# A graph network's second aggregation pair: transposes, own rows and product order rearranged

## The chip, the cores and the metric

The kernel runs on one core of a Trainium2 chip. The metric is the device time of one execution in microseconds (us). One execution was also recorded by the hardware profiler; the profile and the trace are of that execution.

A core has a matrix engine (TensorE, PE in the profile; PEld is its loading of stationary operands), a vector engine (VectorE, DVE), an activation engine (ScalarE, ACT), GpSimd (POOL) and SyncE (SP). Each runs its own list of instructions in order and waits on semaphores for the others. On this kernel SP only issues transfers, and POOL issues the indirect transfers that gather rows. Products are summed in PSUM banks, and an engine has to evict a bank before TensorE may use it again.

## The reference

The input is x (2708 x 512) and a sparse weighted adjacency matrix adj (2708 x 2708, nonzero diagonal). There are four residual layers, each fed by a layer norm. Layer 2, which the change concerns, is a pair of graph convolutions and a dense layer:

```python
h = relu(layernorm(x))
h = relu(adj @ (h @ W1) + b1)
h = relu(adj @ (h @ W3) + b3)
x = x + tanh(h @ Wf + bf)
```

Layer 3 then normalises x, applies relu and `@ W + b`, and averages the result over the nonzero pattern of adj. Layer 0 averages over an incidence matrix, and layer 1 is masked attention over the neighbours.

## The kernel before

Rows are worked on in 22 row tiles of 128 (the last has 20 rows and is called the tail). Low-numbered rows have many neighbours, so each row tile's aggregate is cut in two. WHOLE[m] leading column tiles are multiplied as dense blocks (6 for tiles 0 to 5, 4 or 3 for tiles 6 to 20). The remaining neighbours are listed: CHUNKS[m] chunks of up to 128 columns, whose source rows POOL gathers into eight buffers (L1032) and whose weights are read as `ac` (L1025). Dense blocks are split into a high part, a low part and a sum (a_hi on ACT at L1070, a_lo and a_s on VectorE at L1071 and L1072), so that three quick products each (L1083) give enough precision. A listed chunk is one slow product (L1086). Tile 0 takes all columns as blocks, tile by tile (L1098).

For each row tile of layer 2 the kernel does this:

- Aggregate into two banks, agg (the high products) and aggs (mixed).
- Evict with a bias into u: two VectorE operations at L1117. For tiles 6 to 20 the diagonal is treated alone: the bias is first the tile's own rows times a diagonal weight: SP loads them into u (L1109), VectorE scales them and adds the bias (L1110).
- relu_parts transposes u in four products (L972) and makes v_hi (ACT, L977), v_lo and v_s (VectorE, L978 and L981).
- project3 multiplies these with a weight, in 12 products (L997), into the banks main and mixed, of which there is one each.

There are two loops over row tiles. Stage A (625 to 903 us) is the first aggregation: its projection with W3 is evicted into `go` and stored as g2d, from which the second aggregation gathers. It also stores marks (nz) of what is nonzero, which layer 3 reads. Stage B (903 to 1310 us) aggregates from g2d, projects with Wf, adds bf, applies tanh, and adds the layer's input (L1393 to L1402) to get x after layer 2. It normalises that into z (L189 to L199), transposes z through relu_parts too, projects it with layer 3's W, and stores hid and hidr (L1410, L1413). The adding of a row's own share is L1421. Stage B visits tile 0, 3 to 9, the tail (the tile before 10 in both loops), 10 to 20, and then 1 and 2. Layer 3 follows, from 1310 us; its gathers read hidr, and its masks are the nz marks, read back at L1268.

Each loop body is written for one tile from beginning to end. The order on every engine is decided at build time by a scheduler that moves instructions of neighbouring tiles past each other, within what buffers allow: the pool wp keeps two buffers of each name, among them u (which serves the aggregate, z and the tail's x), v_hi, v_lo, v_s and go; ap keeps two of ac and a_hi, a_lo, a_s; marks have three. TensorE's order before has the eight transposes of one tile's u and an earlier tile's z side by side behind the first dense products of the next tile, and both projections inside them.

Of the kernel before, what the change touches and what calls it, by code (L numbers as in the profile page):

```python
# [14 lines left out]
U8 = mybir.dt.uint8  # L15
# [29 lines left out]
def kernel(  # L45
# [36 lines left out]
    NB = (N + BLK - 1) // BLK  # L82
    UNIT = 4
    assert N % UNIT == 0
    NCH = 8 * ((max(CHUNKS) + 7) // 8)
    NCA = max(CHUNKS)
    NCL = max(CHUNKS[LEAD:])
# [63 lines left out]
    flag = const.tile([P, 1], I32, name="flag")  # L151


    idx_g = const.tile([P, NT, NCH], U32, name="idx_g")

    rdeg = const.tile([P, NT], FP, name="rdeg")
    diag_c, self_w = (const.tile([P, NT], FP, name=name) for name in ("diag_c", "self_w"))
# [81 lines left out]
    with tc.tile_pool(name="l0_slab", bufs=2) as slabs, tc.tile_pool(  # L239
# [177 lines left out]
        def search(m):  # L417

            first = dense_of(m) * P
            num = N - first  # L420
            ranks = ranks_of.pop(m)

            end = wp.tile([P, 1], FP, name="end")
            nc.vector.tensor_scalar_add(end, ranks[:, num - 1 : num], 1.0)
            nc.vector.tensor_copy(ranks[:, num : num + 1], end)
            want = wp.tile([P, NCH], FP, name="want")
            nc.vector.tensor_scalar(want, places, end, None, op0=ALU.min)
            for c0 in range(0, CHUNKS[m], 8):
                c = slice(c0, c0 + 8)
                at = wp.tile([P, 8], U32, name="found")  # L430
                nc.vector.max_index(at, want[:, c], ranks)
                nc.vector.tensor_scalar(
                    idx_g[:, m, c],
                    at,
                    float(N - first),
                    float(first),
                    op0=ALU.min,
                    op1=ALU.add,
                )
                node = wp.tile([P, 8], FP, name="node")  # L440
                nc.vector.tensor_scalar(
                    node,
                    at,
                    float(N - 1 - first),
                    float(N // UNIT),
                    op0=ALU.min,
                    op1=ALU.mult,
                )
                nc.vector.tensor_scalar_add(
                    idx_a[:, m, c], node, float((first * N + m * P) // UNIT)  # L450
                )
            nc.vector.tensor_scalar(
                bad[:, BAD_MANY + m : BAD_MANY + m + 1],
                end,
                float(CHUNKS[m] * P + 1),
                None,
                op0=ALU.is_gt,
            )
# [189 lines left out]
        def gather_rows(m):  # L648

            gs = []  # L650
            for c in range(CHUNKS[m]):
                g = hp.tile([P, D], FP, name=f"h{DENSE + gather_slot[0] % NGG}")
                gather_slot[0] += 1
                nc.gpsimd.indirect_dma_start(  # L654
                    out=g,
                    out_offset=None,
                    in_=h0d[:, :],
                    in_offset=bass.IndirectOffsetOnAxis(ap=idx_g[:, m, c : c + 1], axis=0),
                )
                gs.append(g)  # L660
            gathers[m] = gathers[m], gs
# [282 lines left out]
    order_2 = order_m[:1] + order_m[HEAD:] + order_m[1:HEAD]  # L944
    x3_last = dram.tile([P, D], FP, name="x3_last")

    idx_h = gp.tile([P, NT, NCA], U32, name="idx_h")
    NMARK = DENSE + NCA
    gather_slot = [0]

# [12 lines left out]
    def sum_banks_scaled(dst, main, mixed, n):  # L963

        nc.scalar.activation(dst[:n], main[:n], AF.Copy, scale=SHIFT - 1.0)
        nc.vector.tensor_tensor(dst[:n], mixed[:n], dst[:n], ALU.add)

    def relu_parts(v, n):

        pt = ps_t.tile([P, NCD, P], FP, name="pt")  # L970
        for c in range(NCD):
            nc.tensor.transpose(pt[:, c, :n], v[:n, c * P : (c + 1) * P], ident[:n, :n])  # L972
        hi, lo, s = (
            wp.tile([P, NCD, P], FR, name=f"v_{part}") for part in ("hi", "lo", "s")
        )
# [10 lines left out]
    def project3(parts, n, w, pool=None, names=("main", "mixed")):  # L986

        hi, lo, s = parts
        whi, wlo, ws = w
        main, mixed = ((pool or ps_p).tile([P, D], FP, name=name) for name in names)  # L990
        for acc, a, b, first, last in (
            (main, hi, whi, True, False),
            (main, lo, wlo, False, True),
            (mixed, s, ws, True, True),
        ):
            for c in range(NCD):
                nc.tensor.matmul(  # L997
                    acc[:n],
                    a[:, c, :n],
                    b[:, c, :],  # L1000
                    start=first and c == 0,
                    stop=last and c == NCD - 1,
                )
        return main, mixed

# [15 lines left out]
        return raw[:k, : len(ts), :n], k  # L1021

    def load_listed(m):
        ac = ap.tile([P, NCA, P], FP, name="ac")[:, : CHUNKS[m], : rows(m)]
        nc.sync.dma_start(out=ac, in_=listed[m])  # L1025
        return ac

    def gather(m, gd, gs=None, index=idx_g):

        gs = gs or [gathered() for _ in range(CHUNKS[m])]  # L1030
        for c in range(CHUNKS[m]):
# [1 line left out]
                out=gs[c],  # L1033
                out_offset=None,
                in_=gd[:, :],
                in_offset=bass.IndirectOffsetOnAxis(ap=index[:, m, c : c + 1], axis=0),
            )
        return gs

    def aggregate(m, parts, shifted, gd, marked):  # L1040


        n = rows(m)
# [8 lines left out]
        mixed = ps_a.tile([P, D], FP, name="aggs")  # L1052
        chunks = []
        if num:
            ac = load_listed(m)
            chunks = [(ac[:, c, :], g) for c, g in enumerate(gather(m, gd))]
            if marked:
                mark(whole, ac)
        for ts in ([t for t in ts if t < whole] for ts in dense):
# [15 lines left out]
            for i, t in enumerate(ts):  # L1075
                ghi, glo, gs_ = gs[i]
                first, last = t == 0, t == whole - 1
                for acc, a, b, st, sp in (
# [1 line left out]
                    (main, lo, glo, False, last),  # L1080
                    (mixed, s, gs_, first, False),
                ):
                    nc.tensor.matmul(acc[:n], a[:k, i, :n], b[:k], start=st, stop=sp)  # L1083
        if chunks:
            for c, (a, g) in enumerate(chunks):
                nc.tensor.matmul(  # L1086
                    mixed[:n],
                    a,
                    g,
                    start=(c == 0 and not dense_of(m)),  # L1090
                    stop=(c == len(chunks) - 1),
                )
        else:
            for ts in others:
                gs = [shifted(t) for t in ts]
                raw, k = load_piece(m, ts)
                for i, t in enumerate(ts):
                    nc.tensor.matmul(  # L1098
                        mixed[:n], raw[:, i, :], gs[i][:k], start=False, stop=(t == NT - 1)
                    )  # L1100
        if marked:
            nc.sync.dma_start(out=nonzero[m], in_=nz[:, : whole + num, :n])
        return main, mixed

    def aggregated(m, parts, shifted, gd, bias, marked=False):
        n = rows(m)
        u = wp.tile([P, D], FP, name="u")
        if alone(m):
            nc.sync.dma_start(out=u, in_=gd[span(m)])  # L1109
            nc.vector.scalar_tensor_tensor(  # L1110
                u, u, diag_c[:, m : m + 1], bias, op0=ALU.mult, op1=ALU.add
            )
            bias = u
        main, mixed = aggregate(m, parts, shifted, gd, marked)
        if dense_of(m):
            for bank, scale in ((main, 1.0 - EPS12), (mixed, EPS12)):
                nc.vector.scalar_tensor_tensor(  # L1117
                    u[:n], bank[:n], scale, bias[:n], op0=ALU.mult, op1=ALU.add
                )
                bias = u  # L1120
        else:
            nc.vector.scalar_tensor_tensor(
                u[:n], mixed[:n], EPS12, bias[:n], op0=ALU.mult, op1=ALU.add
            )
        return relu_parts(u, n)

    def g_parts(t):
        return [gp.tile([P, D], FR, name=f"g{part}{t}") for part in ("hi", "lo", "s")]
# [53 lines left out]
    w3 = split_w(wsetb, wr, "wb")  # L1182
    wr = load_w(wset, wf_d, "wr")

    for m in order_m:
        n = rows(m)
        parts = aggregated(m, first_parts, first_product, g1d, bias1, marked=True)
        if m == 0:
            wf = split_w(wset, wr, "wa")
            wr = load_w(wset, w_d, "wr")  # L1190
        main, mixed = project3(parts, n, w3)
        go = wp.tile([P, D], FP, name="go")
        sum_banks_scaled(go, main, mixed, n)
        nc.sync.dma_start(out=g2d[span(m)], in_=go[:n])

    bf = load_bias(bf_d, "bias0")
    bl = load_bias(b_d, "bias2")
# [66 lines left out]
    def gather_h(m):  # L1264
# [1 line left out]
        whole, num = dense_of(m), CHUNKS[m]  # L1266
        nz = marks[m] = ap.tile([P, NMARK, P], U8, name="nz", bufs=3)
        nc.sync.dma_start(out=nz[:, : whole + num, : rows(m)], in_=nonzero[m])  # L1268
        gd, index = (hidr, idx_h) if whole else (hid, idx_g)
        listed_h[m] = gather(m, gd, [next(places_h) for _ in range(num)], index)  # L1270

    def bank_h(m):
        if m not in banks:
# [30 lines left out]
    def listed_products(m):  # L1304
        n = rows(m)
        whole, num = dense_of(m), CHUNKS[m]
        mask = ap.tile([P, NCA, P], FR, name="ac")[:, :num, :n]
        nc.scalar.copy(mask, marks[m][:, whole : whole + num, :n])
        for c, g in enumerate(listed_h.pop(m)):
            high = part_room()  # L1310
# [64 lines left out]
    FIRST = 2  # L1375
    EARLY, FINAL = [list(range(HEAD, DENSE)), list(range(HEAD - 1))], [[HEAD - 1]]
    assert order_2[-1] == HEAD - 1
    for m in order_2:
        n = rows(m)
        parts = aggregated(m, second_parts, second_product, g2d, bias3)  # L1380
        if m == 0:
            w = split_w(wsetb, wr, "wb")
        if dense_of(m) and m not in FULL:
            nc.vector.tensor_scalar_add(
                idx_h[:, m, : CHUNKS[m]], idx_g[:, m, : CHUNKS[m]], float(-HEAD * P)
            )
        if m == order_2[-1]:
            for k in order_3[:FIRST]:
                gather_h(k)
        main, mixed = project3(parts, n, wf)  # L1390
        z = wp.tile([P, D], FP, name="u")
        sum_banks(z, main, mixed, n)
        nc.vector.tensor_add(z[:n], z[:n], bf[:n])  # L1393
        nc.scalar.activation(z[:n], z[:n], AF.Tanh)
        if m == NFULL:
            xt = wp.tile([P, D], FP, name="u")
        else:

            place = {order_2[-1]: "gs0", NSLOT: f"slot{order_2[-1]}"}.get(m, f"slot{m}")
# [3 lines left out]
        if m == NFULL:  # L1403
            nc.sync.dma_start(out=x3_last[:n], in_=xt[:n])
        norm(wp, xt, n, z)
        main, mixed = project3(relu_parts(z, n), n, w)
        go = wp.tile([P, D], FP, name="go")
        sum_banks(go, main, mixed, n)
        nc.vector.tensor_add(go[:n], go[:n], bl[:n])
# [9 lines left out]
            halves[m] = hi, lo  # L1419
        if alone(m):  # L1420
            nc.vector.scalar_tensor_tensor(  # L1421
                xt, go, self_w[:, m : m + 1], xt, op0=ALU.mult, op1=ALU.add
            )

# [460 lines left out]
```

## Time and profile before

| what | value |
|---|---|
| three runs, median (lowest, highest) | 1452.55 us (1449.79, 1455.3) |
| the profiled execution's own time | 1455.42 us |
| its span in the trace | 1453.6 us |
| mean TensorE clock granted | 0.927 of full speed |
| busy: TensorE, VectorE, ScalarE, GpSimd | 85%, 66%, 46%, 45% of the span |
| transfers, mean over the span | 241 GB/s |
| stage A, stage B, layer 3 | 278, 407, 144 us of the span |

The profile's page sums busy time by engine, draws the span in 40 slices, and groups instructions by line. The trace can be asked for the waits of an engine (who was waited for, for how long, how often), for busy time in any stretch, for the chain of work that ended last, and for a timeline of single instructions. TensorE's records have modelled ends that overlap, so its pace is read from the distance between starts: 0.2275 us for a quick 128 x 512 product at full clock, 0.43 at half clock, and 0.857 for a listed chunk, which takes two passes.

### The profile page before, as it was taken

What the parts mean: (1) busy time and instruction counts of PE and PEld (TensorE: products, weight loads), DVE (VectorE), ACT (ScalarE), POOL (GpSimd) and SP (SyncE); (2) the same over time, 40 slices, a digit from 0 to 9 for tenths busy, and PEclk for the clock granted to TensorE, in tenths of its full rate; (3) what the DMA queues carried; (4) which work ended last, traced back from release to release, by engine and by line L of the source; (5) the groups of instructions that cost most, each with busy time, mean ns of one, the idle gap of its engine ahead of it and who ended that gap; (6) DMA issues with size and microseconds to landing.
All of it is one profiled execution on the core that took longest, in us unless ns stands there. A gap on an engine that the chain in (4) does not pass through costs nothing. (4 is left out here: it accounts for less than half of the span.)

```text
span 1453.6 us, 15184 instructions
## 1 busy us (share of the span) xinstructions
PE 1239.6 (85%) x4223; PEld 726.9 (50%) x4223; DVE 954.4 (66%) x2043; ACT 675.0 (46%) x1056; POOL 660.7 (45%) x674
## 2 busy tenths in 40 slices
PE   4888879888778569989998989899988888966997
PEld 2333334334333156655554556466645555555675
DVE  4686998788998478643443356356666656556776
ACT  5875467376344455432312224244444434435563
POOL 1245467666653431055463532334533232265773
PEclk9979999899889779999999989999999999978998
DMA  9989989899794497377776876756746555568995
GB/s 350 341 271 279 304 298 299 304 309 336 220 340 164 152 310 259 103 240 245 253 246 218 265 247 214 259 190 212 215 146 192 155 152 166 167 185 299 275 304 165
DMA packets 187750, 350.68 MB, mean 241 GB/s; under 512 B 22818, under 2 KB 96496, under 8 KB 183925
## 3 DMA queue, kind: packets, MB, share of 16 engines
q1 hardware_dynamic: 140057, 202.48, 41.8%
q0 software_dynamic: 46032, 145.05, 31.3%
q10 hardware_dynamic: 1568, 2.10, 0.4%
q8 instruction: 35, 0.57, 0.2%
q14 instruction: 58, 0.48, 0.1%
HBM read 285.96 MB, written 63.58 MB: 240 GB/s over the span
## 5 line engine op out<-in xcount | busy, mean ns | idle before, releaser
L1032 POOL DMA_INDIRECT gg<-g2d,idx_g x130 | 133.0, 1023 | 242.3 <-PE aggs L1086 199.1
L1086 PE MATMUL aggs<-gg,ac 128*128 128x512 f32 (+1 forms) x520 | 235.8, 595 | 4.7 <-DMA gg<-g1d,idx_g 4.7
L1032 POOL DMA_INDIRECT gg<-g1d,idx_g x130 | 132.3, 1018 | 174.1 <-PE aggs L1086 104.1
L864 PE MATMUL acc<-h,inc 128*128 128x512 f32 (+1 forms) x276 | 149.0, 687 | 47.3 <-DVE inc L704 43.6
L636 POOL DMA_INDIRECT ac<-in_adj_t_dram,idx_a x130 | 129.9, 999 | 101.4 <-issue 32.6
L1086 PEld LDWEIGHTS aggs<-gg,ac 128*128 128x128 f32 (+1 forms) x520 | 97.4, 190 | 104.7 <-issue 93.4
L654 POOL DMA_INDIRECT h<-h0d,idx_g x111 | 112.1, 1010 | 61.5 <-PE acc L864 33.8
L864 PEld LDWEIGHTS acc<-h,inc 128*128 128x128 f32 (+1 forms) x276 | 56.3, 217 | 113.2 <-issue 57.9
L977 ACT ACTIVATE v_hi<-pt 128x512 fp32r<-128x512 f32 (+1 forms) x88 | 48.6, 578 | 132.3 <-PE pt L972 126.3
L1083 PE MATMUL agg<-ghi,a_hi 128*128 128x512 f32 x180 | 86.9, 483 | 24.0 <-DVE u L1117 20.6
L864 PE MATMUL acc<-h,incl 128*128 128x512 f32 (+1 forms) x222 | 101.8, 602 | 0.0
L978 DVE SCALAR_TENSOR_TENSOR v_lo<-pt,v_hi 128x512 fp32r<-128x512 f32 (+1 forms) x88 | 56.7, 665 | 63.2 <-ACT v_hi L977 63.1
L171 PE MATMUL yacc<-wvo,hT 128*128 128x512 f32 (+1 forms) x176 | 84.6, 618 | 4.1 <-ACT hT L206 2.4
L1032 POOL DMA_INDIRECT gg<-hidr,idx_h x62 | 68.8, 1110 | 35.4 <-PE aggs L1283 14.7
L1083 PE MATMUL agg<-glo,a_lo 128*128 128x512 f32 x180 | 78.5, 436 | 4.5 <-ACT glo L220 4.5
L1083 PE MATMUL aggs<-gs,a_s 128*128 128x512 f32 x180 | 73.8, 425 | 2.5 <-DVE gs L217 1.2
L571 ACT ACTIVATE sgn<-ar 128x2708 bf16<-128x2708 f32 (+1 forms) x22 | 54.0, 2456 | 34.3 <-DMA ar<-in_adj_dram 34.3
L997 PE MATMUL main<-wb,v_hi 128*128 128x512 f32 (+1 forms) x176 | 59.1, 461 | 8.7 <-ACT v_hi L977 8.6
L864 PEld LDWEIGHTS acc<-h,incl 128*128 128x128 f32 (+1 forms) x222 | 41.5, 191 | 49.1 <-issue 45.0
L616 DVE MAX8 top<-ar 128x8 f32<-128x2708 f32 (+1 forms) x22 | 65.4, 2971 | 0.0
L618 DVE FIND_INDEX8 at_top<-top,ar 128x8 uint32<-128x2708 f32 (+1 forms) x22 | 65.4, 2972 | 0.0
L1110 DVE SCALAR_TENSOR_TENSOR u<-u,diag_c,bias 128x512 f32<-128x512 f32 x30 | 22.5, 751 | 61.1 <-DMA u<-g1d 46.5
(347 smaller groups left out, 2748.6 us busy)
## 6 DMA issues: line engine op xcount, KB each, us to landing
ar<-in_adj_dram SPq DMA_DIRECT2D x27, 1354.0 KB
raw<-in_adj_t_dram SPq DMA_DIRECT2D x92, 192.0 KB
slot<-x SPq DMA_DIRECT2D x41, 256.0 KB
at<-in_adj_t_dram SPq DMA_DIRECT2D x26, 256.0 KB
h<-in_x_dram SPq DMA_DIRECT2D x21, 256.0 KB
h0d<-h POOLq DMA_DIRECT2D x21, 256.0 KB, 6.9
xt<-in_x_dram SPq DMA_DIRECT2D x21, 256.0 KB
x<-xt SPq DMA_DIRECT2D x21, 256.0 KB
```

Of the source, the lines that this page charges most:

```text
L171: nc.tensor.matmul(acc[:n], hT[:, c, :n], w[:, c, :], start=(c == 0), stop=(c == NCD - 1))
L571: nc.scalar.activation(sgn[:n], ar[:n], AF.Sign, accum_out=sum_sgn[:n])
L616: nc.vector.max(top[:n], ar[:n])
L618: nc.vector.max_index(at_top[:n], top[:n], ar[:n])
L636: nc.gpsimd.indirect_dma_start(out=ac[:, c, :n], out_offset=None, in_=adj_units, in_offset=bass.IndirectOffsetOnAxis(ap=idx_a[:, m, c0 + c ...
L654: nc.gpsimd.indirect_dma_start(out=g, out_offset=None, in_=h0d[:, :], in_offset=bass.IndirectOffsetOnAxis(ap=idx_g[:, m, c : c + 1], axis=0),)
L864: product = nc.tensor.matmul(acc[:n], a, g, start=(i == 0), stop=(i == len(pairs) - 1))
L978: nc.vector.scalar_tensor_tensor(lo[d], pt[d], 0.0, hi[d].bitcast(FP), op0=ALU.max, op1=ALU.subtract)
L997: nc.tensor.matmul(acc[:n], a[:, c, :n], b[:, c, :], start=first and c == 0, stop=last and c == NCD - 1,)
L1032: nc.gpsimd.indirect_dma_start(out=gs[c], out_offset=None, in_=gd[:, :], in_offset=bass.IndirectOffsetOnAxis(ap=index[:, m, c : c + 1], ax ...
L1083: nc.tensor.matmul(acc[:n], a[:k, i, :n], b[:k], start=st, stop=sp)
L1086: nc.tensor.matmul(mixed[:n], a, g, start=(c == 0 and not dense_of(m)), stop=(c == len(chunks) - 1),)
```

## The change

1. While `in_turn` is set, TensorE's instructions of both loops keep the order in which they are written. Stage A, per tile: transposes of the tile before, all dense products, all listed products, projection of the tile before. Stage B runs two tiles longer: transposes of the last u, dense and listed products, transposes of the z of two tiles ago, the Wf projection of the tile before, and the W projection of two tiles ago. Layer 3 and tile 0 of stage A are not pinned.
2. A tile's own rows are loaded into the last four chunks of the `ac` buffer, which is one chunk larger, right behind the list on SP. u no longer holds them.
3. The agg bank is evicted by ACT (a copy with a scale), and VectorE adds the bias; the aggs bank as before.
4. z is kept in a marks buffer (nz, three of them) instead of a u buffer; the tail's x in a go buffer. Its residual add names x3[m] directly.
5. The second index table idx_h goes: idx_g is shifted in place after its last use, and has a column set less.

```diff
+    in_turn = [False]
+    def turn(ins):
+        if in_turn[0]:
+            tc.keep_in_program_order(ins)
     def load_listed(m):
-        ac = ap.tile([P, NCA, P], FP, name="ac")[:, : CHUNKS[m], : rows(m)]
+        both = ap.tile([P, NCA + 1, P], FP, name="ac")
+        ac = both[:, : CHUNKS[m], : rows(m)]
         nc.sync.dma_start(out=ac, in_=listed[m])
-        return ac
+        return ac, both[:, -NCD:, :].rearrange("p c k -> p (c k)")
...
         if num:
-            ac = load_listed(m)
+            ac, spare = load_listed(m)
+            if alone(m):
+                nc.sync.dma_start(out=spare, in_=gd[span(m)])
+                nc.vector.scalar_tensor_tensor(
+                    spare, spare, diag_c[:, m : m + 1], bias, op0=ALU.mult, op1=ALU.add
+                )
+                bias = spare
...
-        if alone(m):
-            nc.sync.dma_start(out=u, in_=gd[span(m)])
-            nc.vector.scalar_tensor_tensor(
-                u, u, diag_c[:, m : m + 1], bias, op0=ALU.mult, op1=ALU.add
-            )
-            bias = u
-        main, mixed = aggregate(m, parts, shifted, gd, marked)
-        if dense_of(m):
-            for bank, scale in ((main, 1.0 - EPS12), (mixed, EPS12)):
-                nc.vector.scalar_tensor_tensor(
-                    u[:n], bank[:n], scale, bias[:n], op0=ALU.mult, op1=ALU.add
-                )
-                bias = u
+        main, mixed, bias = aggregate(m, parts, shifted, gd, marked, bias)
+        if dense_of(m):
+            nc.scalar.activation(u[:n], main[:n], AF.Copy, scale=1.0 - EPS12)
+            nc.vector.tensor_add(u[:n], u[:n], bias[:n])
+            nc.vector.scalar_tensor_tensor(
+                u[:n], mixed[:n], EPS12, u[:n], op0=ALU.mult, op1=ALU.add
+            )
...
+    for i, m in enumerate(order_m):
+        in_turn[0] = i > 0
+        if i:
+            last = order_m[i - 1]
+            near = relu_parts(sums.pop(last), rows(last))
+        sums[m] = aggregated(m, first_parts, first_product, g1d, bias1, marked=True)
...
+        if i:
+            g2_rows(last, near)
+    g2_rows(m, relu_parts(sums.pop(m), rows(m)))
...
-        z = wp.tile([P, D], FP, name="u")
+        z = ap.tile([P, NMARK, P], U8, name="nz", bufs=3).rearrange("p i k -> p (i k)")
+        z = z.bitcast(FP)
...
+    for i in range(NT + 2):
+        if 1 <= i <= NT:
+            last = order_2[i - 1]
+            near = relu_parts(sums.pop(last), rows(last))
+        if i < NT:
+            m = order_2[i]
+            sums[m] = aggregated(m, second_parts, second_product, g2d, bias3)
+            if m == 0:
+                w = split_w(wsetb, wr, "wb")
+            if dense_of(m) and m not in FULL:
+                nc.vector.tensor_scalar_add(
+                    index_g(m)[:, : CHUNKS[m]], index_g(m)[:, : CHUNKS[m]], float(-HEAD * P)
+                )
+        elif i == NT:
+            for k in order_3[:FIRST]:
+                gather_h(k)
+        if i >= 2:
+            far = relu_parts(zs.pop(order_2[i - 2]), rows(order_2[i - 2]))
+        if 1 <= i <= NT:
+            x3_rows(last, near)
+        if i >= 2:
+            hid_rows(order_2[i - 2], far)
+    in_turn[0] = False
```

The new functions g2_rows, x3_rows and hid_rows hold what the loop bodies held: projection, eviction and store. In the changed kernel's order, VectorE reaches an own row's scaling (L1078) right after the eviction of the Wf projection, and issues the sum-bank work of z and hid in turn with the split of u and of the next blocks.

## The prediction

> **What bounds the kernel now.** The page says TensorE leads, and that its clock is not always full:
>
> ```profile
> PE 1239.6 (85%) x4223; PEld 726.9 (50%) x4223; DVE 954.4 (66%) x2043; ACT 675.0 (46%) x1056; POOL 660.7 (45%) x674
> ...
> PEclk9979999899889779999999989999999999978998
> ```
>
> The change touches layer 2 from 625 us to about 1310, so I asked for busy time by stretch. Columns: stretch, length, busy us of PE, PEld, DVE, ACT, POOL, granted clock, DMA share, GB/s.
>
> ```profile
> 625.00:903.00 278.00, 256.17 (x864) 155.36 (x863) 118.33 (x206) 74.10 (x144) 132.08 (x130) 0.95 0.77 247
> 903.00:1100.00 197.00, 185.93 (x666) 116.16 (x665) 115.01 (x216) 78.93 (x121) 80.67 (x80) 0.97 0.65 204
> 1100.00:1240.00 140.00, 119.11 (x431) 79.05 (x430) 88.95 (x161) 58.74 (x85) 43.15 (x41) 0.94 0.54 163
> 1240.00:1310.00 70.00, 55.68 (x197) 37.99 (x196) 39.28 (x82) 30.84 (x45) 33.18 (x33) 0.88 0.57 175
> ```
>
> (1 - clock) times length is work lost to half clock: 13.9, 5.9, 8.4 and 8.4 us. To it come TensorE's waits, by the waits view of each stretch (sum, times, longest). The first three lines are of stage A (625 to 903), the fourth of 1100 to 1240, the last of SP's queue over 903 to 1260:
>
> ```profile
> PE pt L972 <- DVE u L1117: 9.5, 6, 3.0
> PE main L997 <- ACT v_hi L977: 6.4, 1, 6.4
> PE aggs L1086 <- DMA gg<-g1d,idx_g: 4.7, 2, 4.0
> ...
> PE agg L1083 <- DVE u L1117: 20.6, 8, 3.9
> ...
> SPq L1410 <- DVE go L1409: 118.9, 19, 9.2
> ```
>
> All waits: 21.7 us in A; 11.0, 20.8 and 14.3 in B's three stretches. With the clock, A could give up 35.6 us and B's body (903 to 1240) 46.1. B's late waits have one cause, read in the timeline of one tile (start, duration, instruction, idle before):
>
> ```profile
> 1151.99 0.34 SPq L1410 DMA_DIRECT2D hid<-go  x1
> ...
> 1152.90 0.40 SPq L1109 DMA_DIRECT2D u<-g2d  x1
> ...
> 1155.93 0.75 DVE L1110 SCALAR_TENSOR_TENSOR u<-u,diag_c,bias 128x512 f32<-128x512 f32 x1 [1.14 <-DMA u<-g2d]
> ...
> 1157.94 0.50 PE L1083 MATMUL agg<-ghi,a_hi 128*128 128x512 f32 x1 [1.24 <-DVE u L1117]
> ```
>
> The own row's load stands behind the hid store on SP; it lands 3.0 us later, VectorE stalls, evicts the earlier aggregate late, and the next dense product finds its bank occupied. The chain that ended last has this load in every tile; its starts 1116.43, 1135.76, 1152.90, 1170.49, 1187.39, 1205.69, 1222.00 make 105.57/6 = 17.6 us per tile. The matmuls alone, at the 0.2275 us between starts at full clock and 0.857 per listed chunk, are 0.683 x dense + 0.857 x chunks + 24 x 0.2275 + 0.9 (eight transposes): 12.7 us for 3 dense and 5 listed, 14.2 for 4 and 6, 16.5 for 6 and 7.
>
> **What the skill says.** The Trainium skill, "TensorE: Matmul & The Clock Gate", Part 1, halves the clock after an idle window of about 3.4 us; here the wait of 3.0 us in stage A and those of 2.7 to 3.9 around 1140 us are followed by matmuls 0.43 apart, so somewhat shorter waits do it too. The same page, "Engine queue depths", calls VectorE and ScalarE strict FIFOs: the trace agrees, the eviction above sat behind L1110. "DMA: Bandwidth & Descriptors", "Queues, rings and completion order": descriptors of one ring are consumed in order, so the own row will queue behind the list that is now issued before it; the trace before has the other order and cannot show it. "ScalarE: Activation LUTs" puts a table load at about 2.7 us with its drain; the trace has 1.28, and I use that.
>
> **The change, part by part.**
>
> *Own rows.* As many loads (about 0.4 us of SP each) and as many VectorE operations (0.75 us) as before, but issued behind the list of a tile two ahead, no longer behind a hid store. This removes the cause above. New risk: the load lands in the spare chunks perhaps 4 to 6 us after the listed products that freed them (3.0 as measured, plus the list's 320 to 448 KB at the roughly 200 GB/s of the page, 1.6 to 2.2), and L1078 waits for it in VectorE's order, in front of z's bias and the hid eviction, for which TensorE waits a tile later. VectorE reaches L1078 about 4 us after the listed products, so I take no stall, and 1.5 us as the other end.
>
> *Eviction.* Its first half becomes an ACT copy (0.60 us, as L958) and a VectorE add (0.69, as L1393) for 0.68: VectorE unchanged, ACT 0.6 us for each of some 40 tiles, about 25 us hidden in its idle half, except 0.6 in the loop below.
>
> *Pinning, stage A.* Dense and listed products together are 6.3 to 11 us and cover v_hi and v_lo (0.58 + 0.67 + 0.66) of the tile before; 2.75 us of products cover the eviction (about 1.1). Per tile nothing is left to wait for. Uncovered: the first gather (4.0 us, as now), the short tail tile (3 to 5), the two ends (2), and half clock after them (about 5): 15 of 35.6 us stay. Gain 20 us; bounds 5 and 32.
>
> *Pinning, stage B.* z must pass from one x3 product group to the transposes ahead of the next: a loop. From the end of an x3 group, in VectorE's and ScalarE's new order: eviction, own row, bias: 0.2 + 0.69 + 0.75 + 0.69 = 2.4; the hid eviction waits for its products (2.75 + 0.2), then eviction, bias, self, z add: 0.69 + 0.69 + 0.75 + 0.69 to 5.85 (tanh with its table load is done at 4.5); v_lo, statistics, v_s, aggregate 0.67 + 0.68 + 0.66 + 0.17 to 8.1; rstd, then the add of the next u, a_lo and a_s: 0.69 + 0.55 + 0.55 to 9.9; reciprocal and shift to 10.4, normalisation 0.81 to 11.3, semaphore and transposes 0.6, products 2.75: **14.7 us**. A tile whose matmuls are shorter waits for it: three tiles each of 12.7, 13.4, 13.55 and 14.2 us lose 3 x (2.0 + 1.3 + 1.15 + 0.5) = 15 us. These waits of under 2 us should leave the clock alone. The tail tile adds 6, the start (a_hi, raw) 4, some half clock 3: 28 of 46.1 stay; against that some 4 us of small gaps outside the waits go. Gain 22 us; bounds: nothing gained if the own row adds 1.5 us to the loop of its 15 tiles (22 us), 38 gained if ScalarE and VectorE slip past each other better.
>
> *End of B and layer 3.* After the last listed product (1266.9) the last hid product ended at 1309.2, 42.3 us. Now: groups of 2.75 (x3, hid, x3, hid, hid: 13.8), transposes 1.6, sixteen layer 3 products 3.7, two waits for z of about 6 and 8, half clock 4: 37. Gain 5. z lies in the mask buffers, so three mask loads that stood in stage A come at the end of B, ahead of the twelve hid loads instead of behind; the 11.0 us wait at 1337 (mask loads behind hid loads) stays, since the fourth mask still follows them. GpSimd's gathers start from the same hid tile. Layer 3: nothing, bounds -8 and +10. The in-place index shift replaces one of equal size: nothing.
>
> Sum: -20 - 22 - 5 = -47 on the profiled run's own 1455.42 (span 1453.6), which lies 2.9 above the median of the three runs: 1408.4, or 1405.5 on the median's footing; I write 1406.
>
> **Rivals.**
> *Part of the gain goes* (1425 to 1445): the own row lands a microsecond late in the 15 tiles that have one (15 us), or layer 3's masks arrive late (10). For it: SP's queue is in order and its longest waits here are 6 to 9 us. Against: the loads are issued a whole tile ahead. 1406 + 15 + 10 = 1431.
> *Slower* (about 1470): the loop decides. Each us above 14.7 costs one us in some 18 tiles, so at 14.7 + 47/18 = 17.3 us the gain is gone. At 17.5: 18 x 2.8, less 6.6 that the six longest tiles (15.1 and 16.5 us) absorb, makes 44; a dozen waits are then over 2.7 us and cost half of a 3.4 us stretch of half clock each, 20: 1406 + 64 = 1470. For it: VectorE holds some 11.5 us of work in each loop, in strict order, with waits on three other engines and a transfer between. Against: the trace's own durations give 14.7.
> *Better* (about 1385): the scheduler's filling before was worse than I credit, nearly all 82 us but the loop's 15 go: 1452.5 - 67.
> *No change* (within 0.5%, about what a measurement here can tell): layer 3 absorbs everything because POOL sets its end. Against: 80 gathers of about 1.1 us in its 144 us leave POOL idle for a third.
>
> **How the numbers follow.** Main case 0.50 (1390 to 1425), part 0.20, better 0.08, same 0.06, slower 0.16. Faster 0.78. The range 1378 to 1455 leaves about 0.03 below and 0.17 above; the main case alone has 1390 to 1425.
>
> **What would show it.** Right: L1117's role in TensorE's waits gone in B; waits at L972/L986 transposes for ACT's normalisation instead, 0.5 to 2 us in tiles 9 to 20, none in 3 to 8; tile period 14.7 us late in B; clock 0.97 or better from 1100 us on; stage A about 258 us long. Wrong: VectorE waiting at L1078 for the own row by more than 1 us each tile; periods over 17 us; layer 3 longer than 152 us.

## The result and the profile after

The changed kernel takes as long as the one before: 1453.13 us median against 1452.14 in the same measurement, a ratio of 0.9999 with a 95% interval of 0.9976 to 1.0021. The forecast was 1406. Ratios here and below leave out executions in a slower state, while medians are of all executions, so the two can differ by up to 0.7%. The profiled execution of the changed kernel took 1448.14 us of its own, with a span of 1446.3, so its stage times below are some 5 us on the short side of its median.

The time by stages is read from SP's last store of g2d (end of stage A) and of hid (end of stage B). These are the groups of the stores in the two traces: count, durations in ns, first and last start. First the kernel before:

```profile
L1194 SPq DMA_DIRECT2D g2d<-go x22: 301/320/338, 637.8 to 903.9; - x22
L1410 SPq DMA_DIRECT2D hid<-go x22: 283/326/339, 947.2 to 1311.4; - x22
```

The changed kernel:

```profile
L1217 SPq DMA_DIRECT2D g2d<-go x22: 301/329/559, 644.7 to 881.3; - x22
L1446 SPq DMA_DIRECT2D hid<-go x22: 294/319/385, 944.0 to 1301.6; - x22
```

| us | before | after | difference |
|---|---|---|---|
| end of stage A | 903.9 | 881.3 | -22.6 |
| stage B (from there to the last hid store) | 407.5 | 420.3 | +12.8 |
| from the last hid store to the end | 142.2 | 144.7 | +2.5 |

Stage A gave what was forecast (20), layer 3 too (nothing, within 10). Stage B was to become 27 us shorter and became 13 longer. So about 40 us are to be found in stage B. The windows view of the changed kernel has the same columns as before (length, busy PE, PEld, DVE, ACT, POOL, clock, DMA share, GB/s):

```profile
625.00:903.00 278.00, 263.06 (x907) 160.09 (x906) 121.50 (x212) 85.13 (x169) 136.71 (x137) 1.00 0.83 266
903.00:1100.00 197.00, 166.63 (x583) 106.86 (x584) 104.09 (x212) 79.23 (x120) 68.45 (x66) 0.93 0.50 160
1100.00:1240.00 140.00, 126.76 (x477) 84.36 (x475) 94.21 (x184) 69.76 (x103) 48.17 (x45) 0.96 0.52 176
```

From 903 to 1100 us, where the kernel before had been nearly full (185.93 busy, clock 0.97), TensorE now does 83 fewer instructions and its clock is 0.93. Its longest waits there are these (the view for 900 to 1100 us: sum, times, longest). The first and the third are new; for z's normalisation it waited 5.5 us before.

```profile
PE mixed L1013 <- DVE nz L965: 17.7, 6, 3.7
PE pt L986 <- ACT nz L204: 6.2, 2, 4.4
PE main L1013 <- DVE v_lo L993: 4.3, 2, 3.6
```

The wait for L1117, the eviction, is gone as expected. TensorE now waits for VectorE to evict z's banks (L965) and to make v_lo (L993). VectorE's longest wait from 900 to 1250 us says why:

```profile
DVE idx_g L1471 <- DMA gg<-g2d,idx_g: 74.7, 17, 6.3
```

L1471 is the shift of the indices, now in place. It overwrites the indices that a tile's gathers read, so it has to wait until they have landed. It does so 17 times, 4.4 us each. The groups of the shift in both traces show what the forecast took for equal. The kernel before:

```profile
L1384 DVE TENSOR_SCALAR idx_h<-idx_g x17: 156/160/171, 497.7 to 498.8; 128x6 uint32<-128x6 uint32 x6, 128x5 uint32<-128x5 uint32 x6, 128x7 uint32<-128x7 uint32 x5
```

The changed kernel:

```profile
L1471 DVE TENSOR_SCALAR idx_g<-idx_g x17: 170/172/273, 926.0 to 1213.8; 128x6 uint32<-128x6 uint32 x6, 128x5 uint32<-128x5 uint32 x6, 128x7 uint32<-128x7 uint32 x5
```

The same seventeen instructions, equally short. With a table of their own they ran within 1.1 us, ahead of layer 2. In place they are spread over stage B, each in the middle of VectorE's order. One tile of the changed kernel in the timeline (start, duration, instruction, idle before and its releaser):

```profile
1118.69 0.69 DVE L1142 SCALAR_TENSOR_TENSOR u<-aggs,u 128x512 f32<-128x512 f32 x1 [1.34 <-PE aggs L1113]
...
1118.85 0.95 POOL L1050 DMA_INDIRECT gg<-g2d,idx_g  x1 [0.30 <-PE aggs L1113]
...
1124.24 0.17 DVE L1471 TENSOR_SCALAR idx_g<-idx_g 128x6 uint32<-128x6 uint32 x1 [4.86 <-DMA gg<-g2d,idx_g]
1124.32 0.68 DVE L993 SCALAR_TENSOR_TENSOR v_lo<-pt,v_hi 128x512 fp32r<-128x512 f32 x1
...
1125.06 2.08 PE L1013 MATMUL main<-wb,v_lo 128*128 128x512 f32 x4 [2.24 <-DVE v_lo L993]
...
1125.64 0.68 DVE L965 SCALAR_TENSOR_TENSOR nz<-mixed,nz 128x512 f32<-128x512 f32 x1
```

The scheduler has put the shift of the next tile right behind this tile's eviction. The gathers it waits for are issued only as this tile's listed products free their buffers. The last of them is the one at 1118.85 (two more follow until 1121.35, but they are for the tile after, and nothing here waits for them); the shift begins 5.4 us later. VectorE is idle for 4.86 us, with the split of z (L993) and the eviction of the x3 banks (L965) queued behind. From the tail's on, z's transposes start at 1081.61, 1099.84, 1118.48, 1136.21, 1153.08: 17.9 us apart, where the forecast had 14.7. The shift's waits there are 4.65 to 6.10 us. From 1153.08 to 1212.97, where they are 2.04 to 3.88 us, the transposes are 15.0 us apart.

### The profile page after: what moved, and what is told of

It is laid out like the page before. It is cut to its first block, busy times and chain, and to the rows that moved or that the text cites. A ratio compares the mean times of both kernels' runs of the same rounds, so it can differ in the third digit from the quotient of the medians.

```text
span 1446.3 us, 15292 instructions
## 1 busy us (share of the span) xinstructions
PE 1227.4 (85%) x4223; PEld 724.3 (50%) x4223; DVE 946.0 (65%) x2043; ACT 694.9 (48%) x1098; POOL 658.2 (46%) x674
## 5 line engine op out<-in xcount | busy, mean ns | idle before, releaser
L1050 POOL DMA_INDIRECT gg<-g2d,idx_g x130 | 136.6, 1051 | 261.9 <-PE aggs L1113 214.7
L1113 PE MATMUL aggs<-gg,ac 128*128 128x512 f32 (+1 forms) x520 | 232.3, 594 | 2.8 <-DMA gg<-g1d,idx_g 1.7
L1050 POOL DMA_INDIRECT gg<-hidr,idx_g x62 | 67.0, 1081 | 28.5 <-issue 11.0
L1109 PE MATMUL agg<-ghi,a_hi 128*128 128x512 f32 x180 | 77.8, 432 | 0.0
L1109 PE MATMUL agg<-glo,a_lo 128*128 128x512 f32 x180 | 73.0, 406 | 4.8 <-ACT glo L225 4.8
L1142 DVE SCALAR_TENSOR_TENSOR u<-aggs,u 128x512 f32<-128x512 f32 x42 | 28.9, 688 | 68.7 <-PE aggs L1113 68.0
L993 DVE SCALAR_TENSOR_TENSOR v_lo<-pt,v_hi 128x512 fp32r<-128x512 f32 (+1 forms) x88 | 57.9, 663 | 23.3 <-ACT v_hi L992 23.2
L1013 PE MATMUL mixed<-wb,v_s 128*128 128x512 f32 (+1 forms) x176 | 54.0, 433 | 19.5 <-DVE nz L965 19.1
```

Of the source, the lines that this page charges most:

```text
L993: nc.vector.scalar_tensor_tensor(lo[d], pt[d], 0.0, hi[d].bitcast(FP), op0=ALU.max, op1=ALU.subtract)
L1013: nc.tensor.matmul(acc[:n], a[:, c, :n], b[:, c, :], start=first and c == 0, stop=last and c == NCD - 1,)
L1050: nc.gpsimd.indirect_dma_start(out=gs[c], out_offset=None, in_=gd[:, :], in_offset=bass.IndirectOffsetOnAxis(ap=index_g(m)[:, c : c + 1], ...
L1109: turn(nc.tensor.matmul(acc[:n], a[:k, i, :n], b[:k], start=st, stop=sp))
L1113: nc.tensor.matmul(mixed[:n], a, g, start=(c == 0 and not dense_of(m)), stop=(c == len(chunks) - 1),)
```

## The experiments

Two theories stood at the start. Theory 1: the in-place shift holds up VectorE and costs what stage B lost. Theory 2: the loop from z to z or the own rows' landing sets the period, and the shift fills time in which VectorE would wait anyway.

Some chips are slower: there the kernel before has a median of 1522 or 1524 us, and in the traces of e3 to e6, e11 and e12, which ran on them, the first dense product (L1083 in the kernel before) starts at 566 to 580 us instead of 523 to 530. So ratios are to the kernel before on the same chip. The runs e1 and e2 share a chip, as do e3 to e6, e7 to e10, e11 and e12, e13 and e14, and e15 and e16. "The copy" is the changed kernel with the edit of the first experiment.

| run | what differs | median us | ratio to before (95%) |
|---|---|---|---|
| e1_shift_copy | changed kernel, shift writes a copy | 1416.24 | 0.9743 (0.9698 to 0.9789) |
| e2_before_inplace | kernel before, shift in place | 1499.18 | 1.0294 (1.0245 to 1.0342) |
| e3_pins_A_only | copy, stage B unpinned | 1455.86 | 0.9577 (0.9514 to 0.9640) |
| e4_pins_B_only | copy, stage A unpinned | 1484.00 | 0.9713 (0.9643 to 0.9783) |
| e5_own_rows_in_u | copy, own rows and eviction as before | 1461.55 | 0.9539 (0.9460 to 0.9619) |
| e6_hid_late | copy, another pinned order in B | 1450.38 | 0.9532 (0.9483 to 0.9580) |
| e7_after_again | changed kernel | 1456.13 | 1.0016 (0.9997 to 1.0035) |
| e8_copy_again | copy | 1415.93 | 0.9742 (0.9696 to 0.9789) |
| e9_copy_no_pins | copy, no pins | 1393.56 | 0.9572 (0.9533 to 0.9611) |
| e10_hid_late_again | as e6 | 1385.55 | 0.9521 (0.9480 to 0.9563) |
| e11_before_z_in_marks | before, z in a marks buffer | 1514.97 | 0.9905 (0.9861 to 0.9949) |
| e12_before_own_rows_listed | before, own rows behind the lists | 1511.03 | 0.9912 (0.9879 to 0.9944) |
| e13_before_both_moves | before, both of these | 1448.53 | 0.9938 (0.9915 to 0.9962) |
| e14_copy_evict_vector | copy, evictions by VectorE | 1415.12 | 0.9721 (0.9685 to 0.9758) |
| e15_no_pins_own_in_u | as e5, no pins | 1390.36 | 0.9564 (0.9526 to 0.9602) |
| e16_hid_late_no_pins | as e6 (with its pins), one execution | 1384.70 | none |

### The shift: once out of the change, once into the kernel before

The first takes the wait away by writing the shifted indices into columns of the same table that no gather of layer 2 reads (a tile concerned has at most seven chunks). Layer 3's gathers take them from there; that part of the edit is left out here:

```diff
-                    index_g(m)[:, : CHUNKS[m]], index_g(m)[:, : CHUNKS[m]], float(-HEAD * P)
+                    index_g(m)[:, 8 : 8 + CHUNKS[m]],
+                    index_g(m)[:, : CHUNKS[m]],
+                    float(-HEAD * P),
...
```

> The changed kernel, except that the shifted indices are written into columns 8 and up of the same table, which no gather of layer 2 reads, so the shift has nothing to wait for. Theory 1 (the in-place shift, which VectorE reaches before the gathers of the next tile have landed, holds up everything behind it on VectorE): VectorE's 75 us of waits at the shift vanish, TensorE's waits of 31 us at the mixed products and v_lo between 900 and 1250 us fall below 8, tile periods late in stage B fall from 17.7 to about 14.7 us, and the time is 1405 to 1425 us. Theory 2 (the loop from z to z, or the own rows' landing, sets the period, and the shift only fills time in which VectorE would wait anyway): VectorE's waits move to the own row or to the products, periods stay over 17 us, and the time is within 8 us of the kernel before.

The second puts the in-place shift alone into the kernel before, where layer 3's gathers then read idx_g (the second table stays allocated, unused):

```diff
-                idx_h[:, m, : CHUNKS[m]], idx_g[:, m, : CHUNKS[m]], float(-HEAD * P)
+                idx_g[:, m, : CHUNKS[m]], idx_g[:, m, : CHUNKS[m]], float(-HEAD * P)
...
```

> The kernel before with only the index shift done in place, its separate table gone. Theory 1: VectorE gets the same wait for gathers in the order of before, where the shifts had stood ahead of layer 2 with nothing to wait for; TensorE's waits for VectorE grow, and the time rises by 10 to 40 us. Theory 2: the wait falls into VectorE's idle time, and the time stays within 8 us of before.

Theory 1 holds on both sides. Without the wait the changed kernel takes 1416 us. With it alone the kernel before takes 1499, somewhat more than expected: VectorE's waits of that run, from 903 to 1290 us, have

```profile
DVE idx_g L1384 <- DMA gg<-g2d,idx_g: 43.6, 12, 7.5
```

and the same run has TensorE waiting for v_lo and v_s, which it did not before (10.5 and 8.0 us). In the run with the copy the last stores are

```profile
L1217 SPq DMA_DIRECT2D g2d<-go x22: 300/320/558, 639.4 to 879.4; - x22
L1449 SPq DMA_DIRECT2D hid<-go x22: 294/320/384, 937.8 to 1259.2; - x22
```

so stage B has 379.8 us, 27.7 less than before. This trace is of an execution of 1405.74 us, 10.5 below the run's median. In that of e8, an execution of 1412.58 us of the same kernel, stage B has 383.2 us, 24.3 less than before. In e1 z's transposes come at 1067.70, 1082.36, 1096.11, 1112.05, 1126.24, 1141.90, 1156.31, 1171.32 and 1184.21: 116.51/8 = 14.6 us apart (15.3 in e8). The loop of the forecast is there, and TensorE waits where it had to (waits from 1100 to 1250 us):

```profile
PE pt L986 <- ACT nz L204: 10.1, 5, 3.5
```

The runs e7 and e8, on one chip, repeat it:

> The changed kernel as it is, beside the next three on one chip, since chips differ in the stages ahead of layer 2. Theory 1: within 1% of the kernel before, and 2 to 3.5% above the run with the copy.

> The changed kernel with the shift writing a copy, on the same chip. Theory 1: 2 to 3.5% below both.

1.0016 and 0.9742, so the shift in place costs 0.0274 of the 1454.68 us of before on that chip: 40 us. What is left of the change is worth 37 to 38 us by the two ratios of the copy, where the forecast had 47.

### Which part earns the gain

With the shift out of the way, two runs unpin one stage each. They set `in_turn[0] = False` ahead of stage B, or only from there on True.

> The changed kernel with the shift writing a copy (as in the run before), TensorE pinned in stage A only; stage B keeps its new code, own rows behind the lists, z in mask buffers, but the scheduler orders TensorE there. If the pinned order earns the gain of stage B, its last hid store comes 15 to 30 us later than with pins and the time is 1430 to 1450 us. If the own rows alone earn it (they take the wait for the bank away), the time is within 8 us of the pinned one, about 1416.

> The same with TensorE pinned in stage B only. Stage A has the own rows behind the lists and the new eviction, but the scheduler's order. If the pins earn stage A's 24 us, the last g2d store comes at about 904 us as in the kernel before and the time is about 1438. If the own rows earn it, the store comes near 880 us and the time is about 1416.

The next undoes both pieces of the own rows' move (load into u ahead of the list, both evictions by VectorE) and keeps the pins:

> The same with pins in both stages, but own rows loaded into u ahead of the list and evictions by VectorE alone, as in the kernel before. My theory of the kernel before (the own row behind the hid store makes the eviction late) says that the wait comes back, now at the transposes of u, which stand behind one projection only: tile periods late in B of 17 us or more and 1435 to 1460 us. If z's leaving the u buffers already set the load free, within 8 us of 1416.

The last of this group changes the pinned order of stage B. Its core:

```diff
+        def late(i=i):
+            if i >= 3:
+                hid_rows(order_2[i - 3], far)
...
-            sums[m] = aggregated(m, second_parts, second_product, g2d, bias3)
+            sums[m] = aggregated(m, second_parts, second_product, g2d, bias3, between=late)
...
-        if i >= 2:
-            far = relu_parts(zs.pop(order_2[i - 2]), rows(order_2[i - 2]))
         if 1 <= i <= NT:
             x3_rows(last, near)
-        if i >= 2:
-            hid_rows(order_2[i - 2], far)
+        if 2 <= i <= NT + 1:
+            far = relu_parts(zs.pop(order_2[i - 2]), rows(order_2[i - 2]))
```

`between` is called behind the dense products, and the loop runs one iteration longer.

> The same with another pinned order in stage B: the W projection of a tile goes from the end of an iteration to between the dense and the listed products of the next, and z's transposes go behind the Wf projection. The hid eviction then leaves the way from x3 to z, and z has one more projection's time. If that loop (14.6 us late in B, measured) is what remains, periods there fall to 13 to 13.6 us and the time falls by 8 to 18 us below the run with the copy alone, to about 1400. If the own rows' landing or the gathers set the period, it stays at about 1416.

Three of these four went another way, or further, than expected. Unpinning A changes next to nothing (0.9713 against the copy's 0.9742 and 0.9743), which was to speak for the own rows; e15 below, without their move, shows otherwise. So e4 can stand for the copy on this chip, with 1484.00 us. Against it stage B unpinned (e3) is not slower but 28 us faster, own rows back in u (e5) are no loss of 20 to 45 us but 22 us faster, and the late hid order (e6) gains 34 us where 8 to 18 were expected. Once more, beside the copy itself:

> The same with no pins at all: own rows behind the lists, z in mask buffers, the new eviction, and the new code order, with TensorE's order left to the scheduler. If the pins earn half or more of the gain, 10 to 25 us slower than with them. If the own rows earn nearly all of it, within 8 us.

> The copy with the W projection between dense and listed products, beside it on the same chip. If the loop from z to z is what remains of stage B's waits, 8 to 18 us faster than the copy alone; if not, within 5 us.

Without pins 1393.56, with them 1415.93, which neither alternative had; the late hid order gains 30 us over the copy, again more than expected. The timeline without pins shows what they forbid:

```profile
1130.02 4.45 PE L1113 MATMUL aggs<-gg,ac 128*128 128x512 f32 x10
1133.90 1.50 PE L1013 MATMUL main<-wa,v_hi 128*128 128x512 f32 x4
1136.35 0.66 PE L986 MATMUL pt<-ident,nz 128*128 128x128 f32 x4 [0.95 <-ACT nz L204]
1136.77 1.17 PE L1013 MATMUL main<-wa,v_lo 128*128 128x512 f32 x4
```

The order around it is the order that was to be pinned, with one exception: four products of the x3 group, which need nothing of z, stand ahead of z's transposes and fill some 0.9 us of the wait (four times 0.2275). TensorE's waits for z's normalisation sum to 5.6 us from 880 to 1220 us, against 17.1 with pins, and its clock is 0.98 and 1.00 from 1000 to 1100 and 1100 to 1200 us, against 0.95 and 0.97. The late hid order takes z out of TensorE's way all but entirely: 0.5 us. Its longest waits in the same stretch are

```profile
PE aggs L1129 <- DMA raw<-in_adj_t_dram: 4.1, 1, 4.1
PE main L1013 <- ACT v_hi L992: 1.2, 3, 0.7
PE pt L986 <- DVE u L1144: 0.8, 1, 0.8
```

and its median of 1385.55 us is the lowest of those on that chip, though its interval overlaps those of e5, e9 and e15. The same order once more:

> One look more at the pinned order with the W projection between dense and listed products, for its profile on this chip beside the run before it: TensorE's waits between 885 and 1220 us under 10 us in sum, tile periods late in B 13 to 13.6 us.

(This run's label notwithstanding, its order is pinned.) Its one execution took 1384.7 us. z's transposes, from 1034.82 to 1168.23, are 13.3 us apart, and TensorE's waits from 885 to 1220 us sum to 7.6 us.

The pins do not earn the gain, then. Do the two moves out of u? Each alone, and both, in the kernel before (there the shift writes a copy where its table has to go for room):

> The kernel before with only z kept in a marks buffer (and the tail's x in go), so that u's two buffers serve the aggregates alone; own rows still go to u. If the wait for a free u buffer held up the own row's load, the load is issued earlier, TensorE's 20 us of waits for the eviction go, and the time falls by 25 to 55 us (the run with pins and own rows in u points there). If the own row's place behind the hid store on SP is what counts, the time stays within 10 us of before.

> The kernel before with only the own rows moved: into spare chunks of the list's buffer, issued behind the list, evictions still by VectorE; the shift writes a copy; z stays in u. If the own row's place is what counts, 25 to 55 us faster; if the u buffers are, within 10 us of before, since then the eviction still waits for a u that z has not left.

> The kernel before with both moves together (own rows behind the lists, z in a marks buffer) and the shift writing a copy, but its loop bodies, TensorE's order and the evictions as before. If the two buffer moves carry the gain and each alone only bares the other, the ratio is that of the run with the copy and no pins, 0.957, within 0.008. If the new code order (an aggregate written between the transposes of the tile before and their products) carries it, the ratio stays at 0.980 or above.

One per cent each, and 0.6% together. For e11 that is 9 us, for e12 13, between what its two alternatives had named. The wait that the forecast set out from does go: the bank's wait (L1083 for L1117 in the kernel before, 20.6 us) is down to nothing, 1.9 us and nothing in these three. It goes in e11 too: with z out of u alone, an own row's load is issued ahead of the hid store (1168.38 and 1176.36 us), where the kernel before had it behind (1152.90 and 1151.99), so it was z's use of u that had put it there. Other waits take the place of the bank's: over stage B TensorE's waits sum to 45.8 us in the kernel before and to 44.4 in e13. The longest in e13, from 885 to 1260 us, are

```profile
PE pt L972 <- ACT nz L200: 14.1, 9, 3.9
PE main L997 <- DVE v_lo L978: 4.5, 3, 2.7
```

In the old order u and z of two tiles are transposed together and both projections follow at once, so TensorE waits for z in front of all of them. That leaves the new code order, in which an aggregate is written between the transposes of the tile before and their products. The run that keeps of the change only this order and z's buffers, with no pins and with own rows and evictions as before, is

> The changed kernel with the copy, no pins, own rows in u and evictions by VectorE: of the change only the new code order and z in the marks buffers are left. If the code order carries the gain, the ratio to before is 0.945 to 0.965. If the own rows' move is needed beside it, 0.975 or above.

0.9564, the same as with own rows behind the lists and no pins (0.9572). Its last stores are

```profile
L1218 SPq DMA_DIRECT2D g2d<-go x22: 317/355/559, 647.6 to 888.6; - x22
L1449 SPq DMA_DIRECT2D hid<-go x22: 294/320/389, 945.6 to 1240.5; - x22
```

so stage B has 351.9 us, against 403.3 in e13 (903.9 to 1307.2). The scheduler, given loop bodies in this order, comes by itself to nearly the order that was to be pinned. The new code order carries the gain beyond the 1% that z's buffers have alone (e11), in stage A as well: the last g2d store comes at 903.9 us in e13, at 888.6 in e15 and at 883.3 in e9. Whether it would carry it with z still in u was not tried.

Last, which half of the own rows' move costs its 22 us under pins:

> The changed kernel with the copy and all pins, evictions by VectorE alone; own rows stay behind the lists. The run with own rows in u and evictions by VectorE was 2% better than the copy alone. If it is the ACT eviction that costs those 2% (it stands in front of the table load and rstd on the way to z), the ratio to before is 0.95 to 0.96. If it is the own row in front of z's bias on VectorE, it stays at 0.97 to 0.98.

It stays at 0.9721, so the ACT eviction is neutral and the move behind the lists costs it. In the runs with pins VectorE waits for that load (e8, VectorE's waits from 880 to 1220 us):

```profile
DVE ac L1078 <- DMA ac<-g2d: 26.5, 12, 3.1
```

In the tile of 1141 us in the run e1 the load was issued at 1141.16, behind a list, and its scaling began at 1146.94, 5.8 us later; z's eviction stood behind it. Without pins the wait is there too (24.7 us), yet the ratios of e9 and e15 show no cost; that the four products give z the slack is the likely reason, not a tested one. In the late hid order the wait is 3.4 us.

## Why the prediction was wrong

- **The step that failed** is the last line of the part on the end of B: "The in-place index shift replaces one of equal size: nothing." The size is equal, 0.16 and 0.17 us. What changed is what it has to wait for. The copy into a second table waited for no gather of layer 2, and ran at 498 us. The update in place has to wait for every gather that reads the old values, and what stands behind it in VectorE's order waits with it. That was 74.7 us of waiting on VectorE and 40 us of time. The prediction names no such wait. "After its last use", as the change was described, is where the statement stands in the code, behind the tile's listed products; the scheduler had it one tile earlier. The own row's new wait was followed to what is queued behind it; this one was not.
- **Stage B's loop** of 14.7 us measured 14.6 in e1 and 15.3 in e8 once the shift was out, and stage B's gain 27.7 and 24.3 us against 27 (22 in the body and 5 at its end). The agreement is partly luck in its terms: the own row's stall, taken as nothing, was 26 to 28 us of VectorE's time, and without the own rows' move the same pinned order was 22 us faster.
- **"VectorE reaches L1078 about 4 us after the listed products, so I take no stall"** failed too: the load took 5.8 us from its issue in the tile shown, and VectorE waited 2.0 us each time on average (27.7 us in 14 waits in e1), above the 1.5 us of the other end. The forecast's own sign of being wrong, over 1 us at L1078 in each tile, was there, but the shift hid it: in the changed kernel VectorE waited there three times, 5.0 us in sum.
- **Stage A** gained 22.6 us against 20, but not through the pins, to which the forecast gave it. Unpinned it ends at the same time (883.3 us in e9, 884.3 in e8). The order of the code alone, in e15, gave 15 us of it; the rest is little more than the 3 us between two traces of the changed kernel (881.3 and 884.3) and was not traced to a cause.
- **The waits of the kernel before** were measured rightly and weighed wrongly. Taking the bank's wait away, with loop bodies and evictions as before, gave 1%, because other waits, above all that for z, moved into its place.
- **Layer 3** changed by 2.5 us against nothing, within its bounds.
- **The rivals.** "Part of the gain goes" named the own row and the masks, "slower" named the loop reaching 17.3 us as the point where the gain is gone. From 1081 to 1153 us the loop did reach 17.9 and the gain was gone, though the time was that of the kernel before and not 1470; the mechanism that stretched it was not among those named. "These waits of under 2 us should leave the clock alone" was not quite so: of four waits of 1.93 to 2.29 us in e1, from 1052 to 1172 us, that of 1.93 was followed at once by matmuls at half clock (four in 1.97 us instead of 1.17) and that of 2.26 within 1.5 us. This is well below the 3.4 us that the Trainium skill, "TensorE: Matmul & The Clock Gate", Part 1, gives for the idle window. The trace of the kernel before had such a case: after the wait of 1.86 us that ended at 1192.23, products started 0.43 us apart from 1193.36 on.

## What to carry to other kernels

When an edit turns a copy into an update in place, its price can be the wait for the last reader and not the instruction: look up where the scheduler has put it, what it waits for there, and what is queued behind it on that engine. If another order is wanted, try the code order before pinning: here the scheduler came close to the wanted order by itself and kept the freedom to fill a short wait. And a wait removed is worth only the distance to the next one, so name that one before the gain is summed.

## What the runs showed of the hardware

- In this program an update of the index table is held until the gathers that read it have landed, not only until they are issued. In the changed kernel the gather issued at 1100.13 us (0.95 us on POOL) landed 6.0 us later, and the shift that waited for it began at 1106.32.
- A 256 KB load issued right behind a 320 KB list on SP, with two dense blocks of 192 KB just ahead of that, took 5.8 us to the operation that needs it (e1), against 3.0 us for the same load issued behind a store (the kernel before).
- Two chips differ by 5% in the time of the kernel before (1521.81 and 1454.68 us), and the late hid order has nearly the same ratio on both: 0.9532 and 0.9521.
